# Gated cross-attention with routed experts on one core: from block 4 on the queries arrive turned from the host, and the work's places are set anew

## The chip, the core and the metric

The kernel runs on one core of a Trainium2 chip. The core has five engines that run side by side, each in the order of its own instruction queue: TensorE (PE in the profile; its weight loads are PEld), VectorE (DVE), ScalarE (ACT), GpSimd (POOL) and SyncE (SP), which here issues transfers. An engine waits at an instruction until what it needs is there, and everything behind it in the same queue waits too. The metric is the time of one execution in device microseconds; the median of three runs before the change is 1202.55 us (1202.32 to 1202.61).

## The reference

`x` holds 32 sequences of 256 tokens, 256 columns wide; the context has 77 rows per sequence. In short:

```python
x = x + tanh(g_xattn) * attention(layernorm(x), ctx, ctx)   # 16 heads of 16, causal, softmax, @ W.T + b
f = layernorm(x)
shared = swiglu(f @ w_in.T) @ w_out.T                       # hidden 512
h      = swiglu(f @ w1.T)
# two groups of four experts: the better group, in it the two best experts, weights w_se
routed = sum(h * w_se[:, e] @ w2[e].T for e in range(8))
x = x + tanh(g_ffn) * (shared + routed)
```

The layernorm has no weights: `(x - mean) / sqrt(var + 1e-5)`. A query row is such a normalised row; the keys and values are the context itself. The root of a token's variance is one number per query row, so it can be applied to the row of scores instead of to the row of x.

## The kernel before

**Blocks and tiles.** The 8192 tokens are 16 blocks of 512 (two sequences), a block is four tiles of 128 tokens. Everything is fp32.

**Attention, per tile.** `first_stats` takes mean and variance (bn_stats, bn_aggr; L277, L278), once per block `rstd_of` makes the roots (DVE adds EPS, POOL raises to -0.5, L285). `normed` (L290) subtracts the mean and multiplies by the root, tile by tile; `queries` turns two tiles by PE transposes against the identity (L299, names `pt<-ident,xn`), and a copy on ACT (L302, `qT<-pt`) brings them to SBUF. `scores` (L353) multiplies with the keys in groups of 32 rows into `sc`, four PSUM banks with a single buffer; `masked` (L366) adds the mask and brings the scores to SBUF (`ws`, two buffers), `largest` (L378, L379) finds each head's maximum, `exps` (L387) makes 16 exponentials per tile on ACT, one per head, each with its own bias and a running sum. `divided` (L424, L425) divides by the sums on DVE; `transposed` (L440) turns the probabilities, `aT` copies (L443) bring them out, `weighted` (L465) multiplies with the values, `oT` copies, `o_proj` (L485) projects, `residual` (L502) adds x into a second tile `x1`. `biased` (L338, on POOL) has added the output bias to x before. Then `stats2`, `normed2`, `keep` (PE transposes, L299 too, 2 per call) make `xT`, the experts' input.

**Dense work, per block.** `shared` (L790, `ph`), `routed` (L818, `pr`, the record `rec`), `sums` (L842, `pys`). Records go to DRAM, sorted by the pair of experts (`rows<-rec`, by indirect transfers of POOL). Tiles of 128 records of one pair come back (`r_q<-rows`, on SP's queue), are turned (L898, `hp`) and multiplied with the two experts' weights (L905, `py`); the result goes to `out` from POOL. Between, `choice` and `places` find the experts and each record's row, `listing` makes the list of full tiles. 22 tiles or more are left for the end (`finish`).

**The order.** It is written out by hand. The generator `units` yields one unit of dense work after another: a steady block is 28 units, 20 of dense work and two for each of 4 pair tiles. `now` counts units; before and after each half of a unit `due(now)` issues all steps whose place has come. The table `PLACES` gives each step's place relative to the block's start `e` or to `s0 = e - s0 - 3 * gap`; its columns are block 0's four tiles, then blocks 1, 2, 3, 4, 5 to 14, and 15. The attention of block b+1 runs beside the dense work of block b, and its first scores even beside that of block b-1. A step's place sets only where it stands in each engine's queue, not a time.

**Queues and buffers.** SP issues `load` (x, 4 x 128 KB), `load_context` (keys, mask, values), the weights, and `r_q`, in the order of their places; each waits in SP's queue for its buffer. All queues share the core's 16 DMA engines. The PSUM pool `ps` has four banks, which PE fills and ACT or DVE must have emptied before PE can take the bank again. x has three buffers, x1 two, qT one.

The lines that hold the later steps' order of issue in each tile:

```python
        at(p("scores"), lambda: scores(blocks[b], t), pe=True)
        at(p("masked"), lambda: masked(blocks[b], t))
        at(p("weighted"), lambda: weighted(blocks[b], t), pe=True)
```

Of the kernel before, what the change touches and what calls it, by code (L numbers as in the profile page):

```python
# [14 lines left out]
P = 128  # L15
# [20 lines left out]
WIDE = 8  # L36
SURE = 22
# [7 lines left out]
    "s0": (12.5, 17, 20, 12.5, 17, 17, 18, 16, 16.5, 16.5),  # L45
    "gap": (3, 14.5, 3, 3.5, 3, 5, 4, 5.5, 7, 7),
    "stats": (-8, -8, -16, -13.5, -12, -11, -10.5, -9, -8.5, -9),
    "stats_gap": (0.25, 0, -3, -4.25, 0.75, 1.25, 1.25, 1.5, 0.75, 1),
    "bias": (-0.5, -1, -5.5, -8.5, -6, -1.5, -0.5, -1.5, -2.5, -2.5),
    "normed": (-4.5, -3, -5, -3, -3.5, -4.5, -3.5, -4, -4, -5),  # L50
    "normed_gap": (4, 2.75, 1.5, 3.75, 1, 2, 3.25, 1.75, 1.5, 1.75),
    "queries": (-2.5, -3, -5.5, -3.5, -4, -3, -3.5, -4, -3, -4.5),
    "queries_copy": (0, 0.5, -0.5, 3, 0.5, 0.75, 0, 0.75, 0, 1.75),
    "scores": (-2.5, -5, -1.5, -1, -2, -1, -1, 0, -2, -1.5),
    "masked": (0.5, -1.5, -0.5, 0.5, 0.5, 0, 0, 1, 1, 1),
    "largest": (1, 1, 2, 1, 2, 2, 1, 1.5, 2.5, 2.5),
    "exps": (3.5, 4.5, 5.5, 4.5, 3, 3, 2, 3, 3.5, 3),
    "exps_gap": (-1, -1.25, -0.75, -1.5, 0.5, 0.5, 0.5, 0.5, 0.75, 0.5),
    "divided": (5.2, 5.2, 6.2, 5.2, 5.7, 5.2, 4.2, 5.2, 6.7, 6.7),
    "transposed": (8.5, 8, 8, 7.75, 8, 6, 7.5, 7, 8.5, 8.5),  # L60
    "aT": (0.75, 0.5, 1.75, 0.75, 0.25, 0.25, 0, 0.25, 0.5, 0.25),
    "weighted": (9.5, 9.5, 10.5, 9.5, 10, 9, 8, 10, 9.5, 9.5),
    "oT": (0.25, 1.5, 0, 1, 0, 0.75, 1, 0, 0, 0),
    "o_proj": (12, 11, 12.5, 11, 10.5, 10.5, 10, 11, 10, 10),
    "residual": (13, 13, 13.5, 12.5, 11.5, 12, 11, 12, 11, 11),
    "stats2": (13.5, 13.5, 14.5, 13, 12.5, 13.5, 12.5, 13, 12, 12),
    "normed2": (16, 15, 15, 14.5, 14, 14.5, 13.5, 14, 13.5, 13),
    "keep": (16, 15.5, 15.5, 15.5, 14.5, 14.5, 16, 15, 14, 14),
    "xT": (1.25, 1.25, 2.25, 1, 0.25, 0.75, 0, 0, 0.5, 0.5),
    "logits": (10, 12, 15.5, 14.5, -1, -1, 0, -1, -1, -1),  # L70
    "lT": (0, -0.5, -1.25, -2.5, 0.25, 0, 0, 0, 0.25, 0),
    "choice": (11, 10.5, 17, 18.5, 0, 0, 0, -0.5, -0.5, -0.5),
    "choice1": (14, 9.5, 12, 15.5, 1, 1, 1, 0.5, 0.5, 1),
    "choice2": (12.5, 14.5, 10.5, 10.5, 7.5, 2.5, 1.5, 1, 1, 2),
    "choice3": (15.5, 13, 17.5, 14.5, 2, 8.5, 9.5, 2.5, 2.5, 4.5),
    "places": (15.5, 14, 20, 18.5, 3, 3.5, 3, 2, 2.5, 3),
    "places1": (16, 11.5, 11, 3, 4.5, 7, 4, 3.5, 8, 3.5),
    "places2": (16, 17.5, 24, 24.5, 9.5, 5.5, 8.5, 8.5, 4, 7.5),
    "listing": (5, 2, 0, 2.5, 19.5, 9.5, 7.5, 7, 5.5, 5),
    "listing_gap": (2.25, 5, 1.25, 3.75, 1.75, 2, 3, 4.25, 4.75, 4),  # L80
    "load": (-0.5, 2, -2, 0, -10, 9, 4.5, 6, 19.5, 6.5),
    "biased": (-2.5, -2.5, 0, 5, 7.5, 3.5, 5.5, 4.5, 3.5, 11),
    "biased_gap": (2.25, 2.25, 1.5, 2, 0.375, 1.25, 1.75, 2.75, 0.5, 1.25),
    "ends": (9.5, 13.5, 6.5, 11, 5, 10, 7, -3, 11, 6),
    "ends_gap": (2.5, 2, 0, -0.5, 2.25, -2.5, -1, 4.25, 0, 1.75),
    "context": (2, 5, 4, 6.5, -8, 4, -5.5, 0.5, 5.5, 5),
    "shifted": (2, 2, 3, 3.5, -2.5, -1.5, 4.5, -1.5, -5, -13),
    "wide": (4.6, 3.6, 4.1, 4.1, 4, 1.5, 0.5, -0.5, 9, 6),
    "summed": (4.9, 4.9, 4.4, 4.4, -1, 1, -2.5, -9, 5, 0.5),
# [4 lines left out]
def kernel(  # L94
    ctx: ExitStack,
    tc: tile.TileContext,
    x: bass.AP,
    vd: bass.AP,
# [70 lines left out]
    def load(i):  # L169
        s = {"i": i}  # L170
        s["x"] = p3.tile([P, NT, D], F32, tag="x", name=f"x_{i}")
        for t in range(NT):
            nc.sync.dma_start(s["x"][:, t, :], x_v[i][:, t, :])
        return s

# [104 lines left out]
    def rstd_of(var, name):  # L280
        n = var.shape[-1]
        ve = p3.tile([P, n], F32, tag=f"ve{n}", name=f"ve_{name}")
        nc.vector.tensor_scalar_add(ve, var, EPS)  # L283
        rs = p3.tile([P, n], F32, tag=f"rs{n}", name=f"rs_{name}")
        nc.gpsimd.tensor_tensor(rs, ve, nhalf[:, :n], ALU.pow)  # L285
        return rs
# [19 lines left out]
    def first_stats(s, t):  # L306
        if t == 0:
            s["st"] = p2.tile([P, NT, 2], F32, tag="st", name=f"st_{s['i']}")
        stats(s["st"], s["x"][:, t, :], t)
        if s["i"] == 0 and t % 2:  # L310
            s["rs", t // 2] = rstd_of(s["st"][:, t - 1 : t + 1, 1], f"a0_{t}")
        elif s["i"] and t + 1 == NT:
            rs = rstd_of(s["st"][:, :, 1], f"a{s['i']}")
            for k in range(NT // 2):
                s["rs", k] = rs[:, 2 * k : 2 * k + 2]

# [17 lines left out]
    def biased(s, t):  # L334

        assert t < s["normed"]
# [3 lines left out]
    def queries(s, t):  # L340

        if t == 0:
            s["qT"] = p1.tile([P, NC_, TB], F32, tag="qT", name=f"qT_{s['i']}")
        s["qT", t] = turn(s.pop("xq"), s["qT"], t)

    def scores(s, t):
        i, b = s["i"], t // QT
        assert ("qT", t // 2 * 2) not in s
# [26 lines left out]
    def largest(s, t):  # L375
# [3 lines left out]
        nc.vector.tensor_scalar_mul(mx, mx, -(DH**-0.5))  # L379
# [4 lines left out]
    def exps(s, t, heads):  # L384
        s["exps", t] = s.get(("exps", t), 0) + len(heads)
        for h in heads:
            nc.scalar.activation(  # L387
                s["pr", t][:, h, :], s["ws", t][:, h, :SK], AF.Exp,
                bias=s["mx", t][:, h : h + 1], scale=DH**-0.5,
# [104 lines left out]
    def residual(s, t):  # L494
        i = s["i"]
        if t == 0:
            s["x1"] = p2.tile([P, NT, D], F32, tag="x1", name=f"x1_{i}")
            s["st2"] = p2.tile([P, NT, 2], F32, tag="st2", name=f"st2_{i}")
        x1 = s["x1"][:, t, :]
# [708 lines left out]
```

## Time and profile before

| what | value |
|---|---|
| median of three runs | 1202.55 us (1202.32 to 1202.61) |
| the profiled execution | 1204.88 us, span 1203.1 us |
| PE busy | 1158.4 us, 96% of the span |
| DVE, ACT, POOL busy | 898.4, 615.1, 291.6 us |
| one steady block (blocks 4 to 13) | 70.34 to 70.35 us |
| start of block 0's dense work, of block 4, of the last 22 tiles | about 53, 288, 1111 us |

The profile comes from one execution. Its page gives busy time per engine and the costliest groups: line, engine, operation, output and inputs by the program's names, shapes, the number of instructions, then busy us and the mean ns of one, then the idle time of the engine before them and what ended it. A time window repeats the busy times for one stretch. The timeline has instructions in order of time, with neighbours of the same line merged: start, length, engine, line, operation, names, number. Matmuls are pipelined, so lengths overlap and differences of starts are the better measure of what a step costs PE.

### The profile page before, as it was taken

To read this page: it belongs to the slowest core of one execution; us is meant where nothing else is said; L and a number is where in the kernel's file an instruction comes from. 1 tells how busy PE (TensorE), PEld (TensorE's weight loads), DVE (VectorE), ACT (ScalarE), POOL (GpSimd) and SP (SyncE) were. 2 spreads that over 40 slices of the span, in tenths; PEclk is the share of its full clock that TensorE was granted. 3 is DMA by queue.
4 is the path that set the end of the run, shared out by engine and by line. 5 is a ranking of instruction groups with operands and counts; after the bars stand their busy time and mean duration, and the time that the engine had idled before them with its cause. 6 is when DMAs were issued, how large, how long until landed. Compare 5 with 4: busy or idle time off the path is not lost.

```text
span 1203.1 us, 23398 instructions
## 1 busy us (share of the span) xinstructions
PE 1158.4 (96%) x7548; PEld 785.0 (65%) x7548; DVE 898.4 (75%) x2504; ACT 615.1 (51%) x2594; POOL 291.6 (24%) x509
## 2 busy tenths in 40 slices
PE   4799999999999999999999999999999999999997
PEld 3576555556575766767576676757667575757886
DVE  7988979897868688786868878686887868574222
ACT  3875675555555645555564555556455555411110
POOL 2013131222130312313031231302223122224222
PEclk9899999999999999999999999999999999999999
DMA  7102061213131121313112131311213020134442
GB/s 251 40 15 93 15 245 37 71 41 124 40 106 58 67 85 65 112 41 107 58 67 84 58 120 40 102 62 67 84 53 107 28 81 31 46 102 165 126 116 78
DMA packets 39016, 98.89 MB, mean 82 GB/s; under 512 B 6824, under 2 KB 17962, under 8 KB 38384
## 3 DMA queue, kind: packets, MB, share of 16 engines
q1 hardware_dynamic: 28976, 60.78, 16.5%
q0 software_dynamic: 9488, 36.47, 7.7%
q8 instruction: 64, 1.05, 0.4%
q14 instruction: 56, 0.46, 0.1%
q10 hardware_dynamic: 432, 0.13, 0.0%
HBM read 60.50 MB, written 39.74 MB: 83 GB/s over the span
## 4 chain that ended last, share of the span: by engine, by line
PE 69%; issue 6%; POOL 2%; ACT 2%; DVE 1%; POOLq 0%; DVEq 0%; ACTq 0%
PE pr L818 15%; PE py_q L905 15%; PE ph L790 14%; PE pys L842 7%; PE vT L465 4%; PE po L485 3%; PE ptr L440 3%; PE sc L353 3%; POOL out L925 2%; PE pt L299 2%; PE hp_q L898 2%; ACT hT_q L900 1%; PE plT L529 1%; ACT sa L802 1%; ACT aT L443 0%
## 5 line engine op out<-in xcount | busy, mean ns | idle before, releaser
L387 ACT ACTIVATE pr<-ws,mx 128x77 f32<-128x77 f32 x992 | 341.3, 349 | 10.5 <-DVE mx L379 10.0
L790 PE MATMUL ph<-xT,win_sb 128*128 128x512 f32 (+1 forms) x544 | 242.4, 581 | 1.8 <-ACT xT L302 1.0
L818 PE MATMUL pr<-w_sb,xT 128*128 128x512 f32 x512 | 243.1, 603 | 0.7 <-DVE rec L833 0.3
L905 PE MATMUL py_q<-w_sb,hT_q 128*128 x784 | 184.8, 382 | 4.3 <-ACT hT_q L900 4.3
L387 ACT ACTIVATION_READ_ACCUMULATOR pr<-ws,mx 128x1 f32 x992 | 188.9, 190 | 0.0
L905 PEld LDWEIGHTS py_q<-w_sb,hT_q 128*128 128x128 f32 x784 | 143.5, 190 | 25.7 <-ACT hT_q L900 7.4
L790 PEld LDWEIGHTS ph<-xT,win_sb 128*128 128x128 f32 x544 | 97.6, 191 | 87.3 <-issue 72.9
L818 PEld LDWEIGHTS pr<-w_sb,xT 128*128 128x128 f32 x512 | 90.5, 190 | 84.9 <-issue 74.1
L285 POOL TENSOR_TENSOR rs_f<-ve_f,nhalf 128x1 f32<-128x1 f32 x64 | 36.7, 573 | 380.3 <-DVE ve_f L283 356.4
L443 ACT COPY aT<-ptr 124x512 f32<-124x512 f32 (+1 forms) x192 | 86.8, 523 | 71.0 <-PE ptr L440 70.8
L842 PE MATMUL pys<-wout_sb,gT 128*128 128x256 f32 x512 | 121.7, 380 | 0.0
L859 POOL DMA_INDIRECT rows<-rec,posi x64 | 69.2, 1081 | 204.0 <-DVE rec L856 85.6
L842 PEld LDWEIGHTS pys<-wout_sb,gT 128*128 128x128 f32 x512 | 95.6, 190 | 26.0 <-issue 12.6
L925 POOL DMA_INDIRECT out<-acc_q,r_q x49 | 61.5, 1255 | 146.8 <-DVE acc_q L916 120.8
L425 DVE TENSOR_TENSOR pr<-pr,rc 128x1232 f32<-128x1232 f32 x64 | 92.9, 1452 | 2.2
L366 DVE TENSOR_TENSOR ws<-sc,mb 128x1232 f32<-128x1232 f32 x64 | 91.6, 1432 | 2.0 <-PE sc L353 2.0
L378 DVE TENSOR_REDUCE mx<-ws 128x16 f32<-128x1248 f32 x64 | 92.5, 1445 | 0.5
L440 PE MATMUL ptr<-ident,pr 128*124 128x128 f32 x640 | 83.6, 277 | 2.9 <-DVE sr L832 1.1
L440 PEld LDWEIGHTS ptr<-ident,pr 128*124 128x124 f32 x640 | 73.2, 141 | 19.2 <-issue 6.2
L302 ACT COPY xT<-pt 128x256 f32<-128x256 f32 x64 | 23.8, 371 | 116.8 <-PE pt L299 116.8
L905 PE MATMUL py_last<-w_sb,hT_last 128*128 x352 | 79.6, 379 | 0.3 <-ACT hT_last L900 0.3
L828 ACT ACTIVATE sr<-pr 128x512 f32<-128x512 f32 x64 | 38.0, 593 | 78.1 <-PE pr L818 63.6
(181 smaller groups left out, 1577.8 us busy)
## 6 DMA issues: line engine op xcount, KB each, us to landing
r_q<-rows SPq DMA_DIRECT2D x49, 386.0 KB
va<-in_vd SPq DMA_DIRECT2D x16, 640.0 KB
r_last<-rows SPq DMA_DIRECT2D x22, 386.0 KB
x<-in_x SPq DMA_DIRECT2D x64, 128.0 KB
kbd<-in_kbd SPq DMA_DIRECT2D x16, 308.0 KB
w_sb<-in_w2T SPq DMA_DIRECT2D x4, 1024.0 KB
mi<-in_mask SPq DMA_DIRECT2D x16, 77.0 KB
win_sb<-in_w_inT SPq DMA_DIRECT2D x1, 1024.0 KB
```

Of the source, the lines that this page charges most:

```text
L366: nc.vector.tensor_tensor(ws[:, :, :SK].rearrange("p (g h) k -> p g h k", g=RG), s.pop(("sc", t))[:, :, : NC_ * PK].rearrange("p g (h k) - ...
L378: nc.vector.tensor_reduce(mx, s["ws", t], AX.X, ALU.max)
L387: nc.scalar.activation(s["pr", t][:, h, :], s["ws", t][:, h, :SK], AF.Exp, bias=s["mx", t][:, h : h + 1], scale=DH**-0.5, accum_out=s["rc" ...
L425: nc.vector.tensor_tensor(pr, pr, rc.unsqueeze(2).to_broadcast([P, NH, SK]), ALU.mult)
L440: nc.tensor.transpose(pt[:CR, (r - r0) * P : (r - r0 + 1) * P], pr[:, row : row + CR], ident)
L443: s["aTc", t, r0 // 4] = lambda r0=r0, n=n, pt=pt: nc.scalar.copy(aT[:, r0 : r0 + n, :].rearrange("k r q -> k (r q)"), pt[:CR, : n * P])
L790: nc.tensor.matmul(ab[half][:, : n * P], lhsT=win_sb[:, c, f0 : f0 + P], rhs=s["xT"][:, c, cols], start=(c == 0), stop=(c == NC_ - 1),)
L818: nc.tensor.matmul(ab[half], lhsT=s["xT"][:, c, t * P : (t + 1) * P], rhs=w1_sb[:, c, half * HID : (half + 1) * HID], start=(c == 0), stop ...
L842: nc.tensor.matmul(py[:, :D], lhsT=s["g"][:, m, t * P : (t + 1) * P], rhs=wout_sb[:, m, :], start=(m == 0), stop=(m == NM - 1),)
L859: put(nc.gpsimd.indirect_dma_start(out=rows, out_offset=bass.IndirectOffsetOnAxis(ap=s["pos"][:, t, :], axis=0), in_=rec, in_offset=None,), i)
L905: nc.tensor.matmul(py[:, j * D : (j + 1) * D], lhsT=hT[:, m, :], rhs=w2_sb[:, m, bass.ds(e_at[j], D)], start=(m == 0), stop=(m == NM - 1),)
L925: done_with(nc.gpsimd.indirect_dma_start(out=out, out_offset=bass.IndirectOffsetOnAxis(ap=ids, axis=0), in_=acc, in_offset=None, bounds_ch ...
```

## The change

From block 4 on (`OWN = 4`):

- The host passes `xt`, x turned (512 KB per block); `load_turned` brings it to `qT` (two buffers now). `normed`, `queries` and their copies on ACT are no longer issued.
- `lay_out` writes the block's 512 means from `st` to DRAM in token order, `spread` reads them back onto all partitions (256 KB), `centred` subtracts them from `qT` on DVE in one instruction.
- The root is no longer applied to the queries. `rstd_of` multiplies variance plus EPS by 16 before the power, which makes the roots a quarter as large (1/sqrt(16) is the scores' scale); `largest` multiplies by minus this root, and `exps` takes it as the scale, a pointer to one number per partition in place of a constant.

For all blocks: `residual` writes into x's own tile (x1 is gone, x has four buffers), `lT` has one buffer, and most of the table is new. Division stays where it was, on DVE. In the steady column `scores` moves from -2 to -4.5, which puts it right behind the `weighted` of an earlier tile.

```diff
+OWN = 4
 PLACES = {
...
-    "stats": (-8, -8, -16, -13.5, -12, -11, -10.5, -9, -8.5, -9),
-    "stats_gap": (0.25, 0, -3, -4.25, 0.75, 1.25, 1.25, 1.5, 0.75, 1),
+    "stats": (-9.5, -9, -11.5, -4, -8.5, -9.5, -10, -13.5, -12.75, -13.5),
+    "stats_gap": (2.25, 0.75, -1.75, -3.25, 0.5, 1.5, 0.75, 1.5, 0.75, 0.75),
...
-    "scores": (-2.5, -5, -1.5, -1, -2, -1, -1, 0, -2, -1.5),
+    "scores": (-3, -3.5, -1.5, -0.5, -2, -1, -1, 0, -4.5, -1.5),
...
-    "exps": (3.5, 4.5, 5.5, 4.5, 3, 3, 2, 3, 3.5, 3),
-    "exps_gap": (-1, -1.25, -0.75, -1.5, 0.5, 0.5, 0.5, 0.5, 0.75, 0.5),
+    "exps": (3.5, 4.5, 5.5, 4.5, 3, 3, 2, 3, 3, 3),
+    "exps_gap": (-1.25, -1.5, -0.75, -1.25, 0.5, 0.5, 0.25, 0.5, 1, 0.75),
...
-    "o_proj": (12, 11, 12.5, 11, 10.5, 10.5, 10, 11, 10, 10),
+    "o_proj": (12, 11, 12.5, 11, 10.5, 10.5, 10, 11, 10.5, 10),
...
-    "listing": (5, 2, 0, 2.5, 19.5, 9.5, 7.5, 7, 5.5, 5),
+    "listing": (7, 2.5, -2, 5.5, 20, 11.5, 9.5, 7.5, 5.5, 6.5),
...
+    "centred": (5.5, 2, -2, -0.5, 3.5, 8.5, -0.5, -1.5, -6, -3.5),
+    "spread": (-1, -4, 1, 1, -12.5, -10, -10.5, -7, -7.5, -9),
+    "lay_out": (2.5, 4.5, 2.5, -1, -7.5, -13, -8.5, -9, -10, -11),
+    "turned": (4.5, 4, 7, 4, -8, 1, -8, -2.5, -1.5, 0.5),
 }
...
-        s["x"] = p3.tile([P, NT, D], F32, tag="x", name=f"x_{i}")
+        s["x"] = p4.tile([P, NT, D], F32, tag="x", name=f"x_{i}")
...
+    def load_turned(s):
+        i = s["i"]
+        s["qT"] = p2.tile([P, NC_, TB], F32, tag="qT", name=f"qT_{i}")
+        nc.sync.dma_start(s["qT"], xt[i])
...
-    def rstd_of(var, name):
+    def rstd_of(var, name, by=1.0):
...
-        nc.vector.tensor_scalar_add(ve, var, EPS)
+        nc.vector.tensor_scalar(ve, var, EPS, by, ALU.add, ALU.mult)
...
-        elif s["i"] and t + 1 == NT:
+        elif 0 < s["i"] < OWN and t + 1 == NT:
...
+        elif s["i"] and t + 1 == NT:
+            s["rs"] = rstd_of(s["st"][:, :, 1], f"a{s['i']}", DH)
+
+    def lay_out(s):
+
+        assert s["read"] == NT
+        s["means"] = tc.dram_tile([NT, P], F32, name=f"means_{s['i']}")
+        nc.sync.dma_start(s["means"].rearrange("t p -> p t"), s["st"][:, :, 0])
+
+    def spread(s):
+        s["mean"] = p1.tile([P, TB], F32, tag="mean", name=f"mean_{s['i']}")
+        nc.sync.dma_start(
+            s["mean"], s.pop("means").rearrange("t p -> (t p)").partition_broadcast(P)
+        )
+
+    def centred(s):
+        nc.vector.tensor_tensor(
+            s["qT"], s["qT"], s.pop("mean").unsqueeze(1).to_broadcast([P, NC_, TB]), ALU.subtract
+        )
+        s["centred"] = True
...
-        nc.vector.tensor_scalar_mul(mx, mx, -(DH**-0.5))
+        if i < OWN:
+            nc.vector.tensor_scalar_mul(mx, mx, -(DH**-0.5))
+        else:
+            nc.vector.tensor_scalar(mx, mx, -1.0, s["rs"][:, t : t + 1], ALU.mult, ALU.mult)
...
+        scale = DH**-0.5 if s["i"] < OWN else s["rs"][:, t : t + 1]
...
-                bias=s["mx", t][:, h : h + 1], scale=DH**-0.5,
+                bias=s["mx", t][:, h : h + 1], scale=scale,
...
-            s["x1"] = p2.tile([P, NT, D], F32, tag="x1", name=f"x1_{i}")
...
-            x1, s.pop(("po", t))[:, :D], tgx, s["x"][:, t, :], ALU.mult, ALU.add
+            x1, s.pop(("po", t))[:, :D], tgx, x1, ALU.mult, ALU.add
...
+            if b >= OWN:
+                at(begins[b - 2] - place(b, "turned"), lambda b=b: load_turned(blocks[b]))
...
+        if b >= OWN:
+            at(s0 + place(b, "lay_out"), lambda b=b: lay_out(blocks[b]))
+            at(s0 + place(b, "spread"), lambda b=b: spread(blocks[b]))
+            at(s0 + place(b, "centred"), lambda b=b: centred(blocks[b]))
-        for k, t in enumerate(range(0, NT, 2)):
+        for k, t in enumerate(range(0, NT if b < OWN else 0, 2)):
...
+        "xt": x.reshape(NBLK, BB * SQ, NC_, P).transpose(0, 3, 2, 1),
```

In the prediction units are counted from the start of the kernel: block 8's dense work starts at unit 194, block 9's at 222.

## The prediction

> **What bounds the kernel now.** First the page's busy times, for the engine that could be the limit; then the time windows, for whether that engine rests inside a steady block; then the order of time on it, for what each step costs there.
>
> ```profile
> span 1203.1 us, 23398 instructions
> PE 1158.4 (96%) x7548; PEld 785.0 (65%) x7548; DVE 898.4 (75%) x2504; ACT 615.1 (51%) x2594; POOL 291.6 (24%) x509
> ```
>
> ```profile
> 569.70:640.04 70.34, 70.01 (x463) 46.75 (x462) 55.62 (x158) 38.73 (x166) 16.93 (x30) 1.00 0.24 76
> ```
>
> The second line is block 8, from its first `ph` to that of block 9; the columns are the length, then busy PE, PEld, DVE, ACT, POOL, then granted clock, DMA share and GB/s. Of 70.34 us PE is busy 70.01, at full clock; DVE has 14.7 us free and ACT 31.6. Blocks 4 to 13 all repeat in 70.34 or 70.35 us. So a block's time is the sum of PE's instructions, and what is taken off PE there is gained, as long as no operand comes late.
>
> ```profile
> 605.17 1.08 PE L465 MATMUL vT<-aT,va 124*32 124x128 f32 x32
> 606.18 1.98 PE L818 MATMUL pr<-w_sb,xT 128*128 128x512 f32 x4
> 608.00 1.03 PE L485 MATMUL po<-wo_sb,oT 128*128 128x256 f32 x4
> 608.87 1.89 PE L842 MATMUL pys<-wout_sb,gT 128*128 128x256 f32 x8
> 610.59 0.60 PE L299 MATMUL pt<-ident,xn 128*128 128x128 f32 x4
> 611.03 1.88 PE L818 MATMUL pr<-w_sb,xT 128*128 128x512 f32 x4
> 612.84 0.81 PE L353 MATMUL sc<-kbd,qT 32*128 32x154 f32 x16
> 613.58 0.66 PE L299 MATMUL pt<-ident,xn 128*128 128x128 f32 x4
> 614.07 1.88 PE L818 MATMUL pr<-w_sb,xT 128*128 128x512 f32 x4
> 615.79 1.89 PE L842 MATMUL pys<-wout_sb,gT 128*128 128x256 f32 x8
> ```
>
> This is PE's timeline in that block where the next block's queries are turned (start, length, engine, line, names). Durations overlap, so the reader is to subtract starts: the two `pt` groups take 0.44 and 0.49 us, a `pr` 1.72. But the `pr` before `sc` takes 1.81, and the one after `vT` 1.82: passing between the small row-tiled groups (`sc`, `vT`) and the wide ones costs about 0.1 us each way.
>
> ```profile
> L387 ACT ACTIVATE pr<-ws,mx 128x77 f32<-128x77 f32 x992 | 341.3, 349 | 10.5 <-DVE mx L379 10.0 <-DVE bn L277 0.4
> L425 DVE TENSOR_TENSOR pr<-pr,rc 128x1232 f32<-128x1232 f32 x64 | 92.9, 1452 | 2.2
> L290 DVE TENSOR_SCALAR xn<-x,st,rs_a 128x256 f32<-128x256 f32 x64 | 24.9, 417 | 5.9 <-PE pt L299 5.2 <-POOL rs_a L285 0.8
> L302 ACT COPY qT<-pt 128x512 f32<-128x512 f32 x32 | 18.5, 578 | 28.8 <-PE pt L299 28.6
> L802 ACT ACTIVATE sa<-ph 128x512 f32<-128x512 f32 x60 | 35.8, 597 | 63.0 <-PE ph L790 55.0 <-DVE es L624 3.6 <-DVE sa L804 2.8
> ```
>
> These are rows of the groups, shapes kept apart; after the count stand total busy us and mean ns of one.
>
> **What the change takes from PE.** Twelve blocks (4 to 15) lose `queries`: 8 transposes each. In block 8's window, by differences of starts: 0.44 + 0.49, and `pr` 1.81 + 1.72 becomes one run of 8 (3.43, from 575.17 to 578.60 for the same width), so 4.46 becomes 3.43: 1.03 us. The new places also set `scores` right behind `weighted`. `vT` then `sc` occurs early in this trace (starts 121.56, 122.57, 123.31): `vT` 1.01 and `sc` 0.74, no toll between. So each moved `sc` gives back its own two tolls, 0.20 us, and the toll behind `vT` is now paid behind `sc`: two tiles give 0.20 each. The third leaves `places` (`pk`) before wide work, where I take 0.07 (one early `ph` there took 1.88 against 1.82) off its 0.20: 0.13. Sum 1.03 + 0.20 + 0.20 + 0.13 = 1.56 us a block.
>
> Nine windows (blocks 4 to 12) have all of it: 14.0. In block 13's the scores of block 15 keep their place: 1.15. In block 3's and 2's only the transposes go, 0.9 each. Together 17.0 us.
>
> **What it puts on the others.** DVE loses four L290 of 417 ns (1.67 us a block) and gains one subtract over 1024 columns; by L425 that is 1452 x 1024/1232 = 1.21 us. ACT loses two qT copies, 1.16 us. `rstd_of` and `largest` keep their number of instructions; a factor by pointer in one of 16 columns stays near L379's 238 ns.
>
> The exponentials' scale becomes a pointer, 64 per block, 16 in a row. No row has two pointers. From the rows without any (`sa` 256 columns 374 ns, 512 columns 597; `ge` 8 columns 209) 77 columns would be 218 to 269; with the bias pointer and the sum they take 349. So one pointer and the sum cost 80 to 131 ns; a second takes nothing off. Bounds 0 and 131, I take 100, nearer to the pointer's own rows: 6.4 us of ACT a block, 1.6 per tile. Net ACT 38.7 - 1.2 + 6.4 = 43.9 of 68.8. Beside PE it is hidden if each tile's sixteen still end before `divided`. In block 8's window they end at 580.41, DVE takes `divided` up at 582.31; second tile 596.25 and 597.73; third 615.04 (two qT copies in between, now gone) and 616.60; fourth 632.23 and 635.53. Only the second runs out, by 0.1, and there `transposed` follows 2 us after `divided` ends. Taken at nothing; at 131 ns the second tile still holds, by that 2 us.
>
> [...]
>
> **The round trip of the means.** Per block SP now issues the turned input (512 KB), `lay_out` (512 single floats to DRAM), `spread` (256 KB back). SP issues in order, so `lay_out` holds the x loads of the next block until `stats` is through, and `spread` waits for `lay_out` and queues behind those x loads; POOL's queue gets nothing new. Behind them come `context` and the pair tiles' `r_q`, due 14 units (35 us) later. The turned input is issued 11 units ahead, its buffer free since the block before.
>
> From the packet records: `mi` (256 pieces) was issued at 597.00 and its last packet ended at 599.79, 2.8 us; `va` (640 KB) 4.0; the four x loads, behind an `r_q`, 5.0. `lay_out` at 3, then `spread` behind x: 5 after `lay_out` landed at worst, 8 us in all. From the last `stats` (unit 202) to `centred` (206.5) DVE has some 9 us of other work, and `scores` comes 2 us after `centred`. Covered; every us beyond about 11 would be a us of PE per block. The single floats are the unknown: the only 4-byte packets of the trace are completion marks (9 ns). Bounds for `lay_out` are 2.5 us (`kbd`, issued 596.62, last packet ended 599.10) and 4.7 us (a scattered write to DRAM, `out`, issued 569.44, landed 574.13); with either the chain ends below 11. I take no loss. `biased` moves on POOL, but has only `stats` before it and `residual` 8 units behind it.
>
> [...]
>
> **Early blocks and the end.** Until 52.75 us DVE and ACT bind (DVE idle only for `mi`, 2.5 us). Before block 1's first exponentials DVE gets the same set of steps in another order: 0, between -1.5 and +1.5. Block 4's `stats` now stand before the `rec` of units 36 and 38; at 167.27 PE already waits 1.07 us for DVE there, and two `stats` (0.6 each) come in front: +1.2. The wait of 0.38 at 192.29 was a query's: -0.4. The last listing moves 1.5 units later (about 4 us, to 1100); the first `r_last` is held by the last `rows` landing (1099.43) and is used at 1110: 0. x1 becomes x in place, with four buffers: x loads wait less than now.
>
> **Sum.** The profiled execution took 1204.88 us, span 1203.1, 2.3 above the median of 1202.55. -17.0 + 1.2 - 0.4 = -16.2 us. Against the median: 1186.3, I say 1186.5.
>
> **Rivals.** (a) *Part of it turns into new waits.* PE's order is tight: `ptr` already loses 0.2 us in three of four tiles to PSUM banks not yet copied out, and DVE's order is new. Waits of 0.2 to 0.35 per tile, 40 tiles, take back 8 to 14 us: 1194 to 1200. For it: second tile's exponentials without slack. Against: 14.7 us of free DVE, and PE's steady idle of 0.24 us a block.
> (b) *More is gained*: three early waits (1.04, 0.73, 0.57 us) and the bank waits of `ptr` go too, up to 5 us: 1181 to 1183.
> (c) *Slower: the means come late.* Place: `centred`, with `masked` and `rec` queued behind it on DVE, and PE's `scores` behind that. Free up to 11 us, it eats the gain of 1.56 at about 12.6 and decides at 12.8; it needs `lay_out` near 8 us, some 170 ns a float on 32 per queue. At 15 us: 12 x 4 = 48 lost, 17 gained, about 1235. Against it: the 40-byte rows of `wr_sb` took 11 ns a packet, the 616-byte ones of `mi` 32 in the median.
> (d) *The pointer scale costs far more* (250 ns): 4 us a tile, `transposed` late by about 1.5 in two or three tiles, 3 to 4 us a block: about 1210.
> (e) *Nothing moves*: early losses or (a) at its worst, 1200 to 1205; the transposes do go, so it needs an equal new wait.
>
> **Chances and range.** Forecast (1183 to 1190) 0.57, (a) with what lies between 0.21, (b) 0.07, (c) 0.06, (d) 0.05, (e) 0.04. Runs of this kernel differ by 0.02%, and 0.2% (2.4 us) is what I count as a change. Faster: 0.57 + 0.21 + 0.07 = 0.85, and half of (e): 0.87; same 0.02; slower 0.11. The range 1182 to 1197 leaves out (c), (d), (e), the worst of (a) and a part of (b), 2 in 10. The forecast's own range is 1183 to 1190.
>
> **What would show it.** Steady blocks repeating in 68.8 us (69.3 without the tolls, 70.3 or more under (a), 74 under (c)); `pt` with 160 instead of 256 instructions; no PE wait on `centred` or DVE `ws`; exponentials near 445 ns in 768 cases. I am wrong if PE waits for qT, if DVE idles before `centred` for DMA, or if `ptr` waits for `divided`.

## The result, and the profile after

| | before | after | forecast |
|---|---|---|---|
| median time, us | 1202.58 (4 runs, 1202.32 to 1204.21) | 1278.06 (4 runs, 1277.05 to 1280.74) | 1186.5 (1182 to 1197) |
| after / before | | 1.0628, 95% interval 1.0608 to 1.0648 | 0.987 |

The change makes the kernel 6.3% slower. The page after, span and busy times, and two of its groups (after the count: busy us, mean ns of one, idle of the engine before them and what ended it):

```profile
span 1275.3 us, 23238 instructions
PE 1171.1 (92%) x7452; PEld 789.9 (62%) x7452; DVE 904.0 (71%) x2468; ACT 672.1 (53%) x2570; POOL 298.3 (23%) x509
...
L425 ACT ACTIVATE pr<-ws,mx,rs_a 128x77 f32<-128x77 f32 x768 | 335.3, 441 | 80.3 <-DVE mx L415 80.2
...
L386 PE MATMUL sc<-kbd,qT 32*128 32x154 f32 x1024 | 60.2, 355 | 51.2 <-DVE qT L344 46.8
```

PE has 96 matmuls fewer, as it should, and yet it is busy 12.7 us longer and idle 59.5 us more. TensorE's idle time has a name: `sc`, the scores, wait 46.8 us for `qT`. The view of all waits leads one step further back, and the waits of SP's own queue the next (us in total, times, longest):

```profile
DVE qT L344 <- DMA mean<-means: 74.0, 12, 7.8
PE sc L386 <- DVE qT L344: 46.8, 9, 5.6
```

```profile
SPq L339 <- DMA means<-st: 86.5, 11, 9.8
```

So `centred` waits for `spread`, 12 times, and `spread` (L339, on SP) waits for `lay_out`, 86.5 us in 11 blocks. One such place in block 7's window, in order of time over all engines (start, length, engine, line, names; in brackets the idle time before and what ended it):

```profile
550.70 0.38 SPq L335 DMA_DIRECT2D means<-st  x1
...
551.13 2.03 SPq L179 DMA_DIRECT2D x<-in_x  x4
...
558.90 1.43 DVE L399 TENSOR_TENSOR ws<-sc,mb 128x1232 f32<-128x1232 f32 x1
...
560.17 0.33 SPq L339 DMA_DIRECT2D mean<-means  x1
...
562.22 1.08 PE L503 MATMUL vT<-aT,va 124*32 124x128 f32 x32
567.05 1.23 DVE L344 TENSOR_TENSOR qT<-qT,mean 128x1024 f32<-128x1024 f32 x1 [6.72 <-DMA mean<-means]
...
568.34 1.41 PE L386 MATMUL sc<-kbd,qT 32*128 32x154 f32 x16 [5.03 <-DVE qT L344]
...
569.67 3.78 PE L855 MATMUL pr<-w_sb,xT 128*128 128x512 f32 x4
...
573.25 1.73 PE L523 MATMUL po<-wo_sb,oT 128*128 128x256 f32 x4
```

`lay_out` is issued at 550.70 and has landed at 560.17, when SP can issue what waits for it: 9.5 us. `spread` takes 6.9 more. VectorE has work until 560.34, then idles 6.72 us, and TensorE, which needs the centred queries, 5.03. The lines behind the wait tell of a second loss: `sc` takes 1.41 us (0.81 before), the `pr` 3.78 (1.98 before). The time windows show why, in the column behind POOL's busy time, the granted clock:

```profile
526.90:603.90 77.00, 71.63 (x456) 47.79 (x455) 55.79 (x155) 43.48 (x164) 17.98 (x30) 0.96 0.30 80
...
567.80:574.70 6.90, 6.37 (x24) 3.72 (x25) 4.20 (x9) 3.77 (x17) 1.32 (x4) 0.51 0.15 58
```

For 6.9 us, from about the end of the wait, TensorE is given half its clock. The first line is block 7's whole window: 77.0 us where 68.8 were forecast.

By windows, each from the first `ph` of a block to that of the next (for 15, to the first `py` of the last tiles), with the two versions that the experiments led to:

| window of block | before | forecast | after | 16-byte pieces, old listing | and old early places, block 4's stats later |
|---|---|---|---|---|---|
| 0 | 63.45 | 63.5 | 62.11 | 62.13 | 62.09 |
| 1 | 55.80 | 57.0 | 59.46 | 59.49 | 55.81 |
| 2 | 53.00 | 51.7 | 52.88 | 52.54 | 54.21 |
| 3 | 63.10 | 62.2 | 72.47 | 70.75 | 67.92 |
| 4 to 12, mean | 70.36 | 68.8 | 76.45 | 68.80 | 68.81 |
| 13 | 70.34 | 69.2 | 77.27 | 69.36 | 69.36 |
| 14 | 66.21 | 66.2 | 66.21 | 66.21 | 66.21 |
| 15 | 53.53 | 53.5 | 52.82 | 52.82 | 52.82 |

Of the 72.2 us between the two spans, 61.8 lie in the windows of blocks 4 to 13, 9.4 in block 3's.

### The profile page after: what moved, and what is told of

It is laid out like the page before. It is cut to its first block, busy times and chain, and to the rows that moved or that the text cites. A ratio compares the mean times of both kernels' runs of the same rounds, so it can differ in the third digit from the quotient of the medians.

```text
span 1275.3 us, 23238 instructions
## 1 busy us (share of the span) xinstructions
PE 1171.1 (92%) x7452; PEld 789.9 (62%) x7452; DVE 904.0 (71%) x2468; ACT 672.1 (53%) x2570; POOL 298.3 (23%) x509
## 5 line engine op out<-in xcount | busy, mean ns | idle before, releaser
L425 ACT ACTIVATE pr<-ws,mx,rs_a 128x77 f32<-128x77 f32 x768 | 335.3, 441 | 80.3 <-DVE mx L415 80.2
L855 PE MATMUL pr<-w_sb,xT 128*128 128x512 f32 x512 | 256.8, 635 | 5.4 <-DVE sr L869 5.1
L855 PEld LDWEIGHTS pr<-w_sb,xT 128*128 128x128 f32 x512 | 97.5, 200 | 99.4 <-issue 82.3
L827 PEld LDWEIGHTS ph<-xT,win_sb 128*128 128x128 f32 x544 | 97.9, 192 | 87.3 <-issue 75.5
L896 POOL DMA_INDIRECT rows<-rec,posi x64 | 75.8, 1185 | 307.1 <-DVE skip_q L776 97.3
L425 ACT ACTIVATION_READ_ACCUMULATOR pr<-ws,mx,rs_a 128x1 f32 x768 | 145.8, 190 | 0.0
L386 PE MATMUL sc<-kbd,qT 32*128 32x154 f32 x1024 | 60.2, 355 | 51.2 <-DVE qT L344 46.8
L962 POOL DMA_INDIRECT out<-acc_q,r_q x49 | 61.3, 1250 | 130.2 <-DVE acc_q L953 90.2
L386 PEld LDWEIGHTS sc<-kbd,qT 32*128 32x128 f32 x1024 | 43.3, 214 | 69.1 <-DVE qT L344 49.2
```

What stands on the lines that cost most here:

```text
L386: nc.tensor.matmul(sc[:, g, c * PK : (c + 1) * PK], lhsT=s["qT"][rows_, c, t * P : (t + 1) * P], rhs=s["kbd"][rows_, b, c].rearrange("p h ...
L425: nc.scalar.activation(s["pr", t][:, h, :], s["ws", t][:, h, :SK], AF.Exp, bias=s["mx", t][:, h : h + 1], scale=scale, accum_out=s["rc", t ...
L827: nc.tensor.matmul(ab[half][:, : n * P], lhsT=win_sb[:, c, f0 : f0 + P], rhs=s["xT"][:, c, cols], start=(c == 0), stop=(c == NC_ - 1),)
L855: nc.tensor.matmul(ab[half], lhsT=s["xT"][:, c, t * P : (t + 1) * P], rhs=w1_sb[:, c, half * HID : (half + 1) * HID], start=(c == 0), stop ...
L962: done_with(nc.gpsimd.indirect_dma_start(out=out, out_offset=bass.IndirectOffsetOnAxis(ap=ids, axis=0), in_=acc, in_offset=None, bounds_ch ...
```

## The experiments

Theory 1: the round trip of the means is longer than the work beside it, and this wait with the slow clock behind it is the loss of the steady blocks; all else gains as forecast. Theory 2: the exponentials with their second pointer, or VectorE's new order, hold the block, and the wait only marks it. All kernels are edits of the changed one. Eight of them ran on two chips on which the window of block 15 was 6 us longer in every one of them (last experiment of this section). Their times are marked "with the 6 us"; their windows 0 to 14 can be compared as they are.

### The wait taken away, in two ways

```diff
-    "stats": (..., -12.75, -13.5),
+    "stats": (..., -18.75, -19.5),
-    "spread": (..., -7.5, -9),
+    "spread": (..., -13.5, -14.5),
-    "lay_out": (..., -10, -11),
+    "lay_out": (..., -16, -17),
```

> Only places are changed, as against the changed kernel: for blocks 5 to 15 the four stats, lay_out and spread stand 5 to 6 units (about 15 us) earlier; centred, scores and all else stay. Theory 1 (the round trip of the means, 9.4 + 6.4 us, is longer than the work beside it, and that wait with the slow clock behind it is the whole loss): lay_out still takes 8 to 11 us, but mean has landed before centred; PE's wait for qT at scores (46.8 us in all) goes to under 5; steady blocks 68.8 us (68.5 to 69.5), granted clock 0.99 or more, time 1278 - 87 = 1191 (1187 to 1196), faster than before. Theory 2 (the exponentials with a second pointer, or VectorE's new order, hold the block, and the wait only marks it): the wait moves to another place, blocks stay at 72 to 76 and the time at 1230 to 1275.

Measured: 1214.74 us (with the 6 us), 1.0087 of the kernel before (1.0071 to 1.0104). No wait for the means is left: `lay_out` takes 8.3 us (median of blocks 5 to 14, as all such numbers below), the means land 9 us or more ahead of `centred` in these blocks. The blocks go from 76.4 to 70.0. They miss 68.8 by a wait of their own, in TensorE's timeline:

```profile
521.82 1.95 PE L827 MATMUL ph<-xT,win_sb 128*128 128x512 f32 x4 [1.32 <-DVE cnt L698]
```

The `stats` that were moved forward now stand in VectorE's queue ahead of `cnt`, which has to read `pk` out of its PSUM bank before `ph` can go on. TensorE's waits for `cnt` add up to 8.6 us in nine blocks; the blocks lose 1.2 us each.

```diff
-            s["qT"], s["qT"], s.pop("mean").unsqueeze(1).to_broadcast([P, NC_, TB]), ALU.subtract
+            s["qT"], s["qT"], none[:, :TB].unsqueeze(1).to_broadcast([P, NC_, TB]), ALU.subtract
```

> The changed kernel, but centred subtracts a constant tile of zeros in place of the spread means; lay_out and spread are still issued and move the same bytes at the same places. The subtraction of the means is left out, so the queries are not centred. Theory 1: nothing waits for the round trip; blocks 68.8 us, exponentials 441 ns as in the changed kernel, lay_out and spread as slow as there (9 to 11 and about 6 us), time 1191 (1187 to 1196). Theory 2: exponentials or VectorE's order bind, blocks 72 to 76, 1230 to 1275.

Measured: 1202.08 us in one run (with the 6 us). `lay_out` takes 9.2 us as before, and nobody waits for it. A steady block by the time windows:

```profile
570.00:638.80 68.80, 68.47 (x455) 46.15 (x454) 55.66 (x155) 43.34 (x164) 17.96 (x30) 1.00 0.32 89
```

68.80 us at full clock, to the tenth what the prediction's sum over TensorE gave, with the pointer exponentials and the new order in it. Theory 2 is out for the steady blocks. The total misses the 1191 by 11: window 15 is 5.3 us longer than in the kernel before, and windows 0 to 3 are 7.4 us longer than the prediction has them.

### Why lay_out is slow: what lies behind it, or the pieces

```diff
-    "load": (..., 19.5, 9),
+    "load": (..., 16, 9),
```

> Only one place is changed: for blocks 5 to 14 the four x loads are issued 3.5 units later, behind spread, so that nothing stands between lay_out and spread on SP. If the single floats are slow by themselves (Theory 1): lay_out still 7.5 to 10 us, spread 2.5 to 3.5 in place of 6.4, mean 3 to 4 us sooner, VectorE's idle before centred about 3 us, blocks 71 to 73, time 1215 to 1245. If the x loads behind it are what makes lay_out slow: lay_out 3 to 5 us, no wait left, blocks 68.8 and 1191.

Measured: 1267.23 us (with the 6 us), steady blocks 74.1 to 75.5. Without the x loads behind it `lay_out` still takes 8.4 us, 0.8 less than in the kernel above on the same chip (9.2); `spread`, with nothing before it, takes no less than in the changed kernel (5.8 from its issue to its last packet, against 5.5). So the single floats are slow by themselves, as Theory 1 has it, but its second half, that `spread` lost time behind the x loads, was wrong.

```diff
+            s["m"] = p2.tile([P, NT], F32, tag="m", name=f"m_{s['i']}")
+            nc.vector.tensor_copy(s["m"], s["st"][:, :, 0])
...
-        s["means"] = tc.dram_tile([NT, P], F32, name=f"means_{s['i']}")
-        nc.sync.dma_start(s["means"].rearrange("t p -> p t"), s["st"][:, :, 0])
+        s["means"] = tc.dram_tile([P, NT], F32, name=f"means_{s['i']}")
+        nc.sync.dma_start(s["means"], s["m"])
```

> VectorE first copies the four means of a partition side by side, and lay_out writes 128 pieces of 16 bytes in place of 512 of 4; spread and the x loads stay; centred reads the means with a stride. One VectorE copy (about 0.1 us) more per block. If lay_out's time goes by the number of pieces (Theory 1): about 2 + 7.5/4, so 4 us (3 to 5.5), the means landed 5 us sooner, VectorE idle 1 to 2 us before centred in place of 6.7, blocks 69 to 71, time 1192 to 1215. If it goes by the bytes, or by the x loads issued behind it, it stays at 8 to 11 us and the time at 1265 to 1285.

Measured: 1205.29 us in one run (with the 6 us), steady blocks 68.80, no wait for the means. SP's timeline, `lay_out` to `spread`:

```profile
528.13 0.33 SPq L337 DMA_DIRECT2D means<-m  x1
528.52 1.85 SPq L179 DMA_DIRECT2D x<-in_x  x4
530.46 0.39 SPq L341 DMA_DIRECT2D mean<-means  x1
```

2.33 us in place of 9.9: a quarter of the pieces in less than a quarter of the time. And this is no more than SP needs to issue the four x loads in between; the last completion mark of `lay_out` comes 1.4 us after its issue. It may be the pieces' number, their size, or where they lie.

```diff
-        s["means"] = tc.dram_tile([NT, P], F32, name=f"means_{s['i']}")
-        nc.sync.dma_start(s["means"].rearrange("t p -> p t"), s["st"][:, :, 0])
+        nc.sync.dma_start(apart[:, :, 0].rearrange("t p -> p t"), s["st"][:, :, 0])
...
+    apart = tc.dram_tile([NT, P, 16], F32, name="apart")
```

> The changed kernel, but lay_out's 512 single floats go to addresses 64 bytes apart in a DRAM tile that was filled with zeros in the prologue; spread reads the tile's first 512 floats, so that most queries are not centred. Same number of pieces, same size, no two in one 64-byte line. If the number of pieces sets lay_out's time: 8 to 11 us as in the changed kernel (9.9), VectorE idle 6 to 7 us before centred, time 1265 to 1285. If it is that neighbouring floats fall into one line: 2.5 to 4 us, no wait, blocks 68.8, time 1198 to 1208.

Measured: 1203.60 us (with the 6 us), no wait. The same 512 single floats, 64 bytes apart:

```profile
526.75 0.38 SPq L336 DMA_DIRECT2D apart<-st  x1
527.18 2.02 SPq L179 DMA_DIRECT2D x<-in_x  x4
529.30 0.38 SPq L340 DMA_DIRECT2D mean<-apart  x1
```

2.45 us, again SP's own time; the last completion mark comes after 2.1. Neither the number nor the size of the pieces is the cause.

The trace's packets do not tell the two kernels apart. In the changed kernel (block 7, issue at 550.70) as in this one (issue at 526.75) all 512 four-byte packets lie between 0.91 and 1.25 us after the issue, and none lasts over 9 ns. What differs is when the transfer's 16 completion marks come: after 7.2 to 9.4 us there, after 1.6 to 2.1 here.

```diff
+        s["means"] = tc.dram_tile([NT, P, 16], F32, name=f"means_{s['i']}")
+        nc.sync.dma_start(s["means"].rearrange("t p k -> p t k"), s["x"][:, :, 0:16])
```

> The changed kernel, but lay_out writes 512 pieces of 64 bytes (the first 16 columns of x, in place of the means), and spread reads the first 512 floats of them; the queries are centred with wrong numbers. Same number of pieces as in the changed kernel, 16 times the bytes. If the number of pieces sets lay_out's time: 8 to 11 us, time 1265 to 1285. If it is that a piece is smaller than a line: 2.5 to 4 us, no wait, blocks 68.8, time 1198 to 1208.

Measured: 1205.16 us (with the 6 us), no wait; `lay_out` 3.7 us with 32 KB in place of 2. The same answer from the other side.

```diff
-    apart = tc.dram_tile([NT, P, 16], F32, name="apart")
+    apart = tc.dram_tile([NT, P, 4], F32, name="apart")
```

> As the kernel with floats 64 bytes apart, but 16 bytes apart, so that four of the 512 fall into each 64-byte line in place of one (2.45 us) or sixteen (8 to 11 us). If lay_out's time goes by the writes that meet in a line: 2.45 + 3/15 of about 7, so 3.5 to 4.5 us, and no wait. If any two in a line cost the whole: 8 to 11 us, blocks 74 to 77, time 1255 to 1285. If only floats that touch cost: 2.3 to 2.6 us.

Measured: 1196.23 us, no wait; `lay_out` 2.8 to 3.5 us, median 3.13, more than if only floats that touch cost, and a little under what the writes that meet would give:

```profile
525.28 0.38 SPq L336 DMA_DIRECT2D apart<-st  x1
525.71 1.92 SPq L179 DMA_DIRECT2D x<-in_x  x4
528.45 0.33 SPq L340 DMA_DIRECT2D mean<-apart  x1
```

```diff
-        s["means"] = tc.dram_tile([NT, P], F32, name=f"means_{s['i']}")
-        nc.sync.dma_start(s["means"].rearrange("t p -> p t"), s["st"][:, :, 0])
+        s["means"] = tc.dram_tile([P, NT], F32, name=f"means_{s['i']}")
+        nc.sync.dma_start(s["means"], s["st"][:, :, 0])
```

> The changed kernel, but the DRAM tile holds the four means of a partition side by side, with no copy on VectorE; lay_out's source stays strided by 8 bytes, so there are still 512 single floats, sixteen to a 64-byte line, from 4 partitions in place of 16. centred reads with a stride as in the kernel with 16-byte pieces. If the floats in one line are what counts, whoever writes them: 8 to 11 us, a wait, time 1255 to 1285. If it counts that many partitions, and so several DMA queues, write into one line: 2.3 to 4 us, blocks 68.8, time 1198 to 1206.

Measured: 1253.42 us, the wait is back; `lay_out` 7.8 us, just under the 8 to 11:

```profile
545.50 0.53 SPq L335 DMA_DIRECT2D means<-st  x1
546.08 2.04 SPq L179 DMA_DIRECT2D x<-in_x  x4
553.31 0.33 SPq L339 DMA_DIRECT2D mean<-means  x1
```

What `lay_out` takes by the single floats that meet in 64 bytes: 2.1 us with one (to the last completion mark), 3.1 with four, 7.8 with sixteen from 4 partitions, 9.9 with sixteen from 16 partitions (9.2 on another chip). Single floats that fall side by side are the price here, by these four numbers roughly 0.3 to 0.5 us for each that meets another, an estimate; who writes them matters less (7.8 and 9.9). The 16-byte pieces lie four to 64 bytes and show no such price (1.4 us). The tried distances were 4, 16 and 64 bytes. Where between them the border is, and why the completion is late, no run shows; the 64-byte line of the expectations is the author's assumption.

### The pointer of the exponentials

```diff
-        scale = DH**-0.5 if s["i"] < OWN else s["rs"][:, t : t + 1]
+        scale = DH**-0.5
```

(in the kernel with 16-byte pieces)

> The kernel with 16-byte pieces, but the exponentials of blocks 4 to 15 take the constant scale in place of the pointer; the root is left out of the exponent, though not out of its bias. Exponentials 349 ns in place of 441. If the pointer is hidden in the steady blocks, as the prediction has it: they stay at 68.8 us, and only the window of block 3, where PE waits 2.6 us for lT behind block 4's exponentials, gets shorter, 70.7 to 67 or 69; time 1205 to between 1200 and 1204. If the pointer costs there: blocks under 68.5 and time under 1199.

Measured: 1201.52 us (with the 6 us). Time windows of block 3 and of a steady block, first with the pointer (16-byte pieces):

```profile
227.00:297.70 70.70, 62.93 (x410) 37.71 (x411) 56.54 (x157) 38.79 (x151) 16.31 (x29) 0.95 0.21 68
366.50:435.30 68.80, 68.47 (x456) 46.16 (x455) 56.55 (x156) 43.45 (x164) 17.95 (x30) 1.00 0.27 92
```

and with the constant:

```profile
227.50:293.50 66.00, 60.28 (x411) 36.87 (x410) 54.94 (x157) 32.75 (x145) 17.12 (x29) 0.97 0.23 73
362.30:431.10 68.80, 68.47 (x456) 46.14 (x455) 56.46 (x156) 37.93 (x164) 17.79 (x30) 1.00 0.28 92
```

The steady block does not feel the pointer at all; ACT's 5.5 us there are free. Block 3's window does: there block 4's sixteen exponentials stand on ACT in front of `lT`, which TensorE awaits (2.61 us with the pointer, 1.60 without). Of the 4.7 us between the two windows a part is the clock, at half for 6.8 us in the first and for 3.4 in the second. Two other kernels with the pointer and the same places, on the second one's chip, have 68.4 (floats 64 bytes apart) and 69.8 us (64-byte pieces). So the pointer costs 2.4 to 4.7 us there, by one run each.

### The early places, and block 4's stats

```diff
-    "stats": (-9.5, -9, -11.5, -4, -8.5, -9.5, -10, -13.5, -12.75, -13.5),
+    "stats": (-8, -8, -16, -13.5, -12, -11, -10.5, -13.5, -12.75, -13.5),
...
```

(in the kernel with 16-byte pieces; likewise in every row that the kernel before has, columns 0 to 6, which are blocks 0 to 3)

> The kernel with 16-byte pieces, and the places of blocks 0 to 3 as in the kernel before; those of blocks 4 to 15 are the new ones. If the new places of the early blocks cost what the traces show (windows of blocks 0 to 2 together 174.1 us in place of 172.3): these come back to 172 to 173, steady blocks 68.8, the window of block 3 at 66 to 71; time 1205 to between 1198 and 1203, 0 to 0.5% under the kernel before. If the early windows are longer for another reason (x in place, the buffers of x and qT): they stay near 174 and the time near 1205.

Measured: 1204.76 us (with the 6 us), 1.0004 of the kernel before (0.9995 to 1.0014). A miss: windows 0 to 2 give 63.50 + 58.09 + 54.51 = 176.1, more than with the new places (174.1). TensorE waits 1.60 us for block 2's `sr` at 169 us, as in the changed kernel, and the clock falls to half at 169.5. The old places alone don't help, because block 4's `stats` still stand in front of that `sr` on VectorE.

```diff
-    "stats": (-8, -8, -16, -13.5, -12, -11, -10.5, -13.5, -12.75, -13.5),
-    "spread": (-1, -4, 1, 1, -12.5, -10, -10.5, -7, -7.5, -9),
-    "lay_out": (2.5, 4.5, 2.5, -1, -7.5, -13, -8.5, -9, -10, -11),
+    "stats": (-8, -8, -16, -13.5, -12, -11, -10.5, -9, -12.75, -13.5),
+    "spread": (-1, -4, 1, 1, -12.5, -10, -10.5, -3, -7.5, -9),
+    "lay_out": (2.5, 4.5, 2.5, -1, -7.5, -13, -8.5, -4.5, -10, -11),
```

(on top of the last one, and with block 15's listing at its old places, which the next experiment is about)

> As the last kernel, and the places of blocks 0 to 3 as in the kernel before, and block 4's stats, lay_out and spread 4.5 units later (stats at the place of the kernel before). TensorE's wait of 1.6 us for block 2's sr at 169 us, and the slow clock behind it, should be gone if block 4's stats in front of it cause them: windows of blocks 0 to 2 together 172 to 174 us in place of 176.1 with the old places alone. If they do not, 175 to 177. With the listing's effect as above: 1195 to 1199 or 1201 to 1205.

Measured: 1194.74 us (1193.44 to 1196.44), 0.9928 of the kernel before (0.9912 to 0.9945): faster than both kernels. The wait for that `sr` is 1.07 us again, the clock stays full in window 1, and the window is 55.8. Windows 1, 3, 8 and 15:

```profile
114.30:170.10 55.80, 52.81 (x370) 31.23 (x368) 47.38 (x124) 35.17 (x159) 12.93 (x28) 1.00 0.19 68
224.30:292.20 67.90, 61.66 (x410) 36.70 (x409) 53.26 (x150) 38.88 (x152) 16.31 (x29) 0.97 0.23 76
567.60:636.40 68.80, 68.47 (x456) 46.16 (x455) 56.52 (x156) 43.45 (x165) 17.98 (x30) 1.00 0.27 89
1047.10:1099.90 52.80, 52.19 (x193) 33.32 (x189) 32.49 (x112) 8.30 (x17) 21.59 (x32) 1.00 0.34 123
```

What it still misses of the forecast lies in the windows of blocks 2 and 3: 54.2 in place of 51.7, and 67.9 in place of 62.2, with the wait for `lT` (2.69 us) and one half-clock stretch.

### The window of block 15

```diff
-    "listing": (7, 2.5, -2, 5.5, 20, 11.5, 9.5, 7.5, 5.5, 6.5),
-    "ends": (8, 13.5, 7.5, 15, 7.5, 12.5, 9, -0.5, 18.5, 8.5),
-    "ends_gap": (3.25, 2, 0.25, 0.5, 3.25, -1, -0.75, 4.25, -1, 0.25),
+    "listing": (7, 2.5, -2, 5.5, 20, 11.5, 9.5, 7.5, 5.5, 5),
+    "ends": (8, 13.5, 7.5, 15, 7.5, 12.5, 9, -0.5, 18.5, 6),
+    "ends_gap": (3.25, 2, 0.25, 0.5, 3.25, -1, -0.75, 4.25, -1, 1.75),
...
```

(in the kernel with 16-byte pieces; block 15's column alone, and so for its choice and places)

> The kernel with 16-byte pieces, and of block 15 alone the steps of the choice, of the places, of the last listing and of its ends as in the kernel before: the twelve writes to the lists' ends stand 2.5 units earlier and spread out again, in place of twelve in a row on POOL. Open is the window of block 15's dense work: 53.5 us before and 52.8 in the changed kernel, but 59 in each kernel without the wait for the means. If the new places of the listing are behind that: window 52.5 to 54.5, time 1205 to 1198 (1196 to 1200), 0.3 to 0.6% under the kernel before. If not: window 58 to 60, time 1203 to 1206.

Measured: 1197.36 us (1196.41 to 1198.35), 0.9943 of the kernel before (0.9926 to 0.9959); window of block 15 52.8. That would have settled it, had not its neighbours on the same chip had the same window:

> The changed kernel unaltered, beside the two above, to see its last windows under the same conditions. If its window of block 15 is 52.8 us again: the 6 us belong to the kernels that reach it without the waits. If it is 58 to 60: they come from outside the kernel, and the fixed kernels are to be judged without them. Steady blocks 75 to 78, time 1274 to 1284.

Measured: 1260.55 us, window of block 15 52.8, steady blocks 74.1 to 75.9, `lay_out` 9.2 us. Time and blocks miss the forecast: on this chip the unaltered changed kernel is 17.5 us faster than in the first measurement. `lay_out` is shorter, and TensorE's waits in blocks 4 to 13 add up to 40.3 us in place of 51.9. Against the kernel before on the same chip it is 4.7% slower.

> The kernel before unaltered, beside the three above. Window of block 15 53.5 us as before if the 6 us belong to the kernels with the change; 55 to 60 if they come from outside. Time 1202 to 1206.

Measured: 1204.75 us, window of block 15 52.8.

> The fastest version so far, but block 15's listing and ends again at the changed kernel's places; beside its twin below, under the same conditions. If these places delay the end of block 15's dense work: window 58 to 60 us here and 52.8 in the twin, time 5 to 7 us above the twin's. If the 6 us come from outside the kernel (another chip): the two windows are equal, at 52.8 or at 58 to 60.

> The fastest version unaltered, as the twin of the kernel above: window of block 15 52.8 us, time 1193 to 1197, if the places decide; 58 to 60 us and 1199 to 1203 if it is the chip.

Measured: 1193.40 us with the new listing, 1196.49 with the old, the windows 52.82 and 52.83. On this chip the listing's places do nothing to that window, and what the run before seemed to tell is not shown. On two chips, all eight kernels with the change had 58.7 to 60.0 us there; on two others, all eight kernels (the unaltered one before among them) 52.8. In the long windows VectorE starts up to 3.4 us later than the matmuls that it waits for are over in TensorE's own records (in the kernel that subtracts zeros, `pys` is over at 1080.18 and `rec` starts at 1083.60). Why stays open. The kernel before was timed on all four chips: 1204.53 (7 runs) and 1203.61 us (13 runs) on the two with the long window, 1203.85 (7 runs) and 1203.50 (1 run) on the two others. So it does not pay the 6 us; they take those chips and something of the change. That this is the new listing after all is not ruled out, for every kernel with the change that ran on those two chips had it. The fastest version did not run there. The 3 us between the twins lie in windows 0 (62.1 and 63.5, a half-clock stretch more) and in what comes before it.

## Why the prediction was wrong, point by point

**TensorE's sum: right.** "1.56 us a block" gave 68.8; where the wait is gone and nothing else was moved in these blocks, they repeat in 68.8, in eleven kernels. Block 13 with 1.15 less was forecast at 69.19 and is 69.36.

**The step that failed: "`lay_out` at 3, then `spread` behind x: 5 after `lay_out` landed at worst, 8 us in all ... I take no loss."** `lay_out` takes 9.9; `spread` takes 5.5 to its last packet in place of 5; the whole chain takes 16.4 (550.70 to 567.05). Both bounds for `lay_out`, 2.5 and 4.7 us, lay below: they came from rows whose pieces were larger or stood apart, and no row of before had floats side by side. The experiments show that this is what mattered: floats 64 bytes apart land within 2.45 us, and then the step would have been right. The doubt that the prediction had written down pointed there, the single floats as "the unknown". Their number, though, is not what costs here: 512 pieces of one element brought no wait when their targets lay 64 bytes apart.

Two readings behind this step were off. `mi` has 128 pieces in the packet records, not 256. And completion marks are not the only 4-byte packets of the trace before: 256 pieces of `tgx` and `tgf` are too, at most 9 ns each. They are reads of DRAM, though, and the time of a single packet, which the prediction also held against (c) ("11 ns a packet"), bounds nothing: the packets of the slow `lay_out` last no longer than those of the fast one, at most 9 ns in both.

**The cover: right.** "Some 9 us of other work" on VectorE is 9.6 (550.71 to 560.34). By the prediction's own "every us beyond about 11 would be a us of PE", 16.4 costs 5.4 a block; TensorE's wait is 5.2 in the mean of blocks 4 to 13 (51.9 us in ten waits).

**The rival (c) was what happened**, with its place and its chain. Its condition, "`lay_out` near 8 us", was met, and it had 6 chances in 100. Two of the prediction's signs of being wrong are there: TensorE waits for `qT`, and VectorE idles before `centred` for a DMA. Its time, 1235 at a chain of 15 us, would be 1250 at 16.4. It lacked the clock: each of these ten waits of 4.5 to 5.7 us came with half-clock work, 2.5 us more a block (76.5 - 68.8 - 5.2), 25 us in ten blocks.

**The pointer: right in size, wrong in place.** Estimated at 100 ns, it costs 92 (441 against 349). "Taken at nothing" holds in the steady blocks, which alone had been looked at; in block 3's window it takes 2.4 to 4.7 us.

**The early blocks: a wait missed.** "+1.2" for block 4's `stats` in front of block 2's `sr`: the wait grows from 1.07 to 1.59 us, 0.5 in place of 1.2, and is 1.07 again when they are moved. But window 1 lost 3.7 in all. Most of that is a wait that the prediction did not have: for `oT` at 126 us, 1.04 us before and with the old early places, 2.16 with the new ones, and followed by half-clock work (window 1 and 127.1 to 130.5, with 16-byte pieces and the old listing):

```profile
114.50:174.00 59.50, 54.29 (x370) 31.93 (x368) 49.75 (x130) 35.20 (x160) 13.31 (x31) 0.97 0.19 65
127.10:130.50 3.40, 3.39 (x4) 1.51 (x5) 3.20 (x12) 0.00 (x0) 0.00 (x0) 0.50 0.00 0
```

"Transposes go, 0.9 each" in windows 2 and 3: window 2 is 0.1 us shorter in the changed kernel, 0.5 with 16-byte pieces, and 1.2 longer with the old early places; in window 3 waits and the clock bury it. Nothing of the change is shown at the two ends. Window 0 is 1.3 us shorter, but it goes by whether its start falls at half clock (63.5 and 62.1 us in the twins above), as it did in the profile of before. Block 15's window is 0.7 shorter, but the kernel before has 52.8 there too when it is profiled again; the last 91.7 us are the same.

With 16-byte pieces, the old early places and block 4's `stats` moved, the change does bring a gain on this chip, about 9 us (1203.85 to 1194.74) of the 16 that were forecast.

## What to carry to other kernels

A transfer that nothing in the profile resembles in where its pieces land, not only in their number and size, has no bound from above; ask what the schedule costs if it takes three times the highest row, and try it alone first. Take its time from its completion, not from its packets (up to 9.4 us and 1.25 us here). The single floats that went side by side into DRAM (9.9 us) were better gathered on an engine to whole pieces (1.4 us, and 0.16 us of VectorE), or written 64 bytes apart (2.1 us). And a wait on TensorE, where it is otherwise full, costs more than its length if the clock falls with it: here 5.2 us of wait and 2.5 us of slow work a block.

## What the runs showed of the hardware

In the changed kernel 512 single floats written to neighbouring addresses in DRAM took 9.9 us from issue to landing (median of blocks 5 to 14); with the floats 64 bytes apart the last completion mark came after 2.1. The packet records show nothing of it (in block 7 all are over after 1.25 us in both); it is the completion marks that come late, after 7.2 to 9.4 us against 1.6 to 2.1.

In the changed kernel's profile, from 120 us to the end of block 15, TensorE's granted clock is at half (0.50) in 13 stretches of 3.4 or 6.8 us, each of which begins during a wait of TensorE or up to 1.6 us after it. Waits of 1.59 us or less never brought it; those of 2.16, 2.61 and 2.80 us brought 3.4 us of it, and of the ten of 4.5 to 5.7 us nine brought 6.8 and one 3.4. The length alone does not decide. The wait of 1.59 or 1.60 us for block 2's `sr` brought it in five kernels of thirteen (not in the changed kernel, but at 169.5 us with 16-byte pieces and the old early places), the one of 2.59 to 2.62 us for `lT` in three of ten (the changed kernel is one, at 233.3 us). What decides, no run here explains.

The spread of 2 KB onto 128 partitions (256 KB) took 3.2 to 4.3 us from its issue to its last packet in the kernels with fast writes (median of blocks 5 to 14), and 5.1 to 5.8 behind the slow writes. Without the x loads right before it in the queue it took no less (5.8 us, against 5.5 in the changed kernel).
